# Turns by squares and DRAM, a full-width second product and merged transfers in a macaron block of two layers

## The chip, the cores and the metric

The kernel runs on one core of one Trainium2 chip. The metric is the device time of one execution in microseconds; a lower time is better. A core has a matrix engine (PE, whose weight loads are listed as PEld), a vector engine (DVE), a scalar engine for activation functions (ACT), a general engine (POOL) and an engine that in this kernel issues all transfers (SP). Each engine works through its own instructions in order and waits on semaphores for the others.

## The reference

The input x is 8 batches of 256 tokens of 128 numbers, all in float32. Six residual blocks follow one another, each behind a layer norm:

```
x = x + 0.5 * soft_moe(norm(x))
x = x + linear_attention(norm(x))
x = x + 0.5 * soft_moe(norm(x))
x = x + 0.5 * ternary_ffn(norm(x))
x = x + favor_attention(norm(x))
x = x + 0.5 * ternary_ffn(norm(x))
```

- `soft_moe` normalizes again and forms logits of each token against 16 x 64 slots. A softmax over the tokens of a batch mixes the tokens into slots ("dispatch"); each of the 16 experts computes `(gelu(slots Wg + bg) * (slots Wu + bu)) Wd + bd` on its 64 slots of each batch; a softmax over all 1024 slots of a token mixes the experts' outputs into the token ("combine").
- `linear_attention` has 16 heads of 8, `elu + 1` as feature map, sums of keys and values over the tokens of a batch, a division and a projection.
- `favor_attention` has 16 heads of 8 with 32 random features each: a projection, a maximum over the 32, an exponential, sums over the tokens, a division and a projection.
- `ternary_ffn` widens to 512, takes silu times a linear part, then two layers of 512 x 512 with gelu, then goes back to 128.

## The kernel before

**Tiling.** x stays in SBUF, with tokens on the 128 partitions and two tiles (TT = 2) for each batch. The eight batches form two groups of four (`group`, L1366). In a group two layers follow one another: `dispatch` for each batch, `experts` over the 16 experts for all four batches at once, `combine` for each batch and, in the first layer, `linear` for each batch. Behind that come `glu` (the ternary network, for batches in pairs), `favor` and `glu` again. A matmul in float32 appears in the profile as two instructions; a turn of a block as one.

**Order of the work.** The kernel is written as steps. A step (`step`, L90) names its cost on the engines that may run it, its reads and writes, and the buffers it takes. A planner (`Plan.place`, L123) runs once, when the program is built: it goes through the steps with these costs, chooses engine, start and buffer slot for each, and so fixes one order of instructions for each engine. Its priorities are the amount of PE work ahead of a step, moved by a list of numbers (`SHIFTS`), with the second group behind the first by a constant. The two groups thus interleave on every engine. Where the planner sees PE idle for over 0.7 us, it puts some multiplications by an identity before the next step (`idle`, L1399). SP issues every transfer in the planned order; a transfer that has to wait holds all that stand behind it on SP.

**Turning a tile.** Matmuls contract over partitions, so tiles with tokens on partitions must be turned, that is, transposed. The kernel has two ways. `flip` (L375) lets PE turn a block of 128 x 128 into PSUM, from where ACT or DVE evacuates it (`evacuated`, L384 on DVE, L382 on ACT). `squares_turned` (L440) lets DVE turn every square of 32 x 32 (L446), writes the tile to DRAM with one transfer (the spill, L449) and reads it back with four, one for each set of 32 partitions, so that the squares come to stand in their turned places (the placing, L455). Before the change, `linear`, `glu` and one of the operands of `favor` are turned by squares; the normalized y of `dispatch`, the maxima in `dispatch`, the attention output in `project` (L888) and the sums in `favor` go by `flip`.

**dispatch (L594).** It normalizes x into y and turns y (`transposed`, L465), with scale and bias of the norm put on in the evacuation (L493 on ACT, L495 on DVE). `replicated` (L573) spills y to DRAM with four transfers (L579) and reads it back with four (L586) in another order of tokens, copied to each set of 32 partitions. Eight products give the logits (L615); the maximum over slots of a token is folded from them (L632, L708). Then PE turns the maxima, DVE reduces them (L719), PE spreads them over all partitions, and an evacuation gives `mb`, which POOL subtracts from the logits (L737) before the exponential (L743). The softmax over tokens has its own path (L649 to L678) and ends in the products that fill the slots (L691).

**experts (L749).** For each expert, SP fetches one row of weights (L764, 384 KB) into one of four buffers; for every second expert it also fetches the bias bd of the pair with two transfers (L767). The first products (L787) give gate and up part (L793 on ACT, L798 on DVE). The second product (`back`, L818) works on a pair of experts together: each matmul has 64 columns of the array for 64 slots, the even expert on the first half of the array and the odd one on the second, and the bias addition (L830 on DVE) writes its result where `combine` reads it. The results share their memory with the slots. It stands one pair behind the first products.

**combine (L852)** gathers with eight products of 129 columns for each tile (L859).

Of the kernel before, what the change touches and what calls it, by code (L numbers as in the profile page):

```python
# [13 lines left out]
P = 128  # L14

SHIFTS = (
    -2751, -1692, -1691, -12195, -784, -1588, -17523, -441, -1660, -895, -929, -659, -543, -591,
    -517, -633, -219, -357, -610, -370, -144, -340, -138, -261, -103, -124, -149, -112, -87,
    328, -365, -173, -179, -134, 14, 40, -32, 136, -182, -43, -162, -672, 13, -20, 26, 13, -393,
    -13, -49, 76, 108, 25, -337, -106, -98, -405, -124, -14, 106, -15, -91, -232, -26, -141, 72,  # L20
    179, -149, -60, -56, -94, -291, -910, -397, 168, -109, -149, -2, -601, -150, 12, -21, -762,
    -20, -100, 231, -63, -522, -971, -639, -490, -1134, 34, -143, -240, -1126, 30, 98, 272,
    -229, -245, 48, 535, -647, -666, -418, 7, 144, -282, -73, 220, 168, 36, -1118, -353, -720,
    -886, -200, -34, 24, 100, 11, -24, 70, 30, -50, -121, 47, 25, 9, -51, 143, -939, -125, -300,
    -662, -491, -371, -203, -437, -21, -285, -479, -125, 412, 243, 49, 284, 369, 566, -147,
    -339, 157, 267, -173, -269, 162, -518, -492, 53, 116, -414, -523, -222, -451, -400, -304,
    -82, 145, -77, -134, -36, -467, -865, -141, -372, -407, -524, -134, 12, 58, -154, 246, 41,
    -111, 22, 62, -756, -131, 38, -435, -1331, -683, -948, -2046, -2339, -2000, -3450, -2514,
    -3516, -3317, -2307, -1684,
# [187 lines left out]
def macaron_kernel(ctx: ExitStack, tc: tile.TileContext, i: dict, out: bass.AP):  # L217
# [222 lines left out]
    def squares_turned(z, n, cells, dst, out):  # L440


        flat = lambda: z()
        there = dram.tile([P, n // 32, 32], F32, tag=f"t{len(turns)}", name=f"t{len(turns)}")
        turns.append(there)
        step({"DVE": 58 + 1.07 * n}, lambda _: nc.vector.transpose(z(), z()), cells, cells)  # L446

        def spill(_):
            nc.sync.dma_start(there.rearrange("p k j -> p (k j)"), z())  # L449
# [10 lines left out]
        step({"SP": 475}, spill, cells, [there.name], lag=1.5 * n)  # L460
        step({"SP": 2000}, place, [there.name], out, lag=2.5 * n)
# [3 lines left out]
    def transposed(y, n, affine=False, squares=False):  # L465

        yt = Buf("k1" if n == TT else "k2", (P, n * P))
        if squares:
            squares_turned(
                lambda: y.ap[:, 0:n].rearrange("p t d -> p (t d)"), n * P,  # L470
                [(y, t) for t in range(n)], lambda: yt.ap, [yt],
            )
            return yt
# [1008 lines left out]
```

## Time and profile before

| | |
|---|---|
| median of 3 runs | 741.02 us (740.77 to 742.02) |
| the profiled execution | 743.85 us, span 742.1 us |
| PE busy | 728.8 us, 98% |
| DVE busy | 517.2 us, 70% |
| ACT busy | 410.7 us, 55% |
| POOL busy | 306.1 us, 41% |
| bytes moved | 62.34 MB, 30.6% of the 16 DMA engines' time |
| mean granted TensorE clock | 0.998 |

"Busy" is time in which an engine executes. PE's matmuls are pipelined: the mean of one (275 ns with 128 columns) is longer than the distance between two starts, so a group's price is read from the start of the group to the start of the next. "Idle before" is time for which the engine stood before an instruction of that line, with whoever ended it. The planner's orders of both programs are known before anything runs, and with them the number of instructions of each kind and what stands between two of them on an engine.

### The profile page before, as it was taken

To read this page: it belongs to the slowest core of one execution; us is meant where nothing else is said; L and a number is where in the kernel's file an instruction comes from. 1 tells how busy PE (TensorE), PEld (TensorE's weight loads), DVE (VectorE), ACT (ScalarE), POOL (GpSimd) and SP (SyncE) were. 2 spreads that over 40 slices of the span, in tenths; PEclk is the share of its full clock that TensorE was granted. 3 is DMA by queue.
4 is the path that set the end of the run, shared out by engine and by line. 5 is a ranking of instruction groups with operands and counts; after the bars stand their busy time and mean duration, and the time that the engine had idled before them with its cause. 6 is when DMAs were issued, how large, how long until landed. Compare 5 with 4: busy or idle time off the path is not lost.

```text
span 742.1 us, 15296 instructions
## 1 busy us (share of the span) xinstructions
PE 728.8 (98%) x5814; PEld 609.5 (82%) x5814; DVE 517.2 (70%) x1103; ACT 410.7 (55%) x774; POOL 306.1 (41%) x419
## 2 busy tenths in 40 slices
PE   8999999998999999999999999999999999999998
PEld 7878888997889988889878879788687677878787
DVE  6999965577868798975564274455998978855442
ACT  4889967257665577884553240433555664363331
POOL 7989446133427752459910022000745545211000
PEclk9999999999999999999999999999999999999999
DMA  5553432333330526333631210200344244120100
GB/s 143 150 140 118 139 93 94 109 81 97 126 114 2 146 83 197 99 94 119 171 99 52 85 29 1 57 0 15 78 114 95 42 118 81 32 60 14 42 1 29
DMA packets 102105, 62.34 MB, mean 84 GB/s; under 512 B 73104, under 2 KB 88848, under 8 KB 102032
## 3 DMA queue, kind: packets, MB, share of 16 engines
q1 hardware_dynamic: 102032, 61.36, 30.6%
q8 instruction: 46, 0.75, 0.4%
q14 instruction: 27, 0.22, 0.1%
HBM read 49.80 MB, written 11.53 MB: 83 GB/s over the span
## 4 chain that ended last, share of the span: by engine, by line
PE 87%; DVE 5%; DMA 3%; SPq 2%; issue 1%; POOL 1%; ACT 1%; POOLq 0%
PE ps L1077 27%; PE ps L787 14%; PE ps L818 8%; PE ps L859 8%; PE ps L691 6%; PE ps L615 4%; PE ps L1177 4%; PE ps L1147 4%; PE ps L1150 4%; PE ps L375 2%; DMA we<-in_We 1%; PE ps L1256 1%; DVE k L632 1%; PE ps L1307 1%; PE ps L1341 1%; PE ps L907 1%
## 5 line engine op out<-in xcount | busy, mean ns | idle before, releaser
L787 PE MATMUL ps<-slots,we 128*128 128x256 f32 x512 | 121.8, 384 | 4.0 <-DMA we<-in_We 2.3
L787 PEld LDWEIGHTS ps<-slots,we 128*128 128x128 f32 x512 | 94.7, 191 | 20.1 <-issue 5.2
L1077 PE MATMUL ps<-comb,slots 128*128 128x256 f32 x448 | 103.1, 381 | 0.0
L1077 PE MATMUL ps<-comb,comb 128*128 128x256 f32 x448 | 102.5, 381 | 0.0
L1077 PEld LDWEIGHTS ps<-comb,slots 128*128 128x128 f32 x448 | 83.6, 190 | 15.4 <-issue 3.9
L1077 PEld LDWEIGHTS ps<-comb,comb 128*128 128x128 f32 x448 | 83.6, 190 | 13.6 <-issue 2.5
L737 POOL TENSOR_TENSOR comb<-comb,k 128x1024 f32<-128x1024 f32 x32 | 75.1, 2369 | 33.5 <-DVE k L384 14.0
L793 ACT ACTIVATE k<-ps,small 128x256 f32<-128x256 f32 x128 | 56.5, 475 | 48.4 <-PE ps L787 46.1
L382 ACT COPY k<-ps 128x512 f32<-128x512 f32 (+2 forms) x55 | 28.5, 519 | 93.8 <-PE ps L1077 83.1
L670 POOL TENSOR_TENSOR comb<-comb,sm 128x1024 f32<-128x1024 f32 x32 | 60.9, 1911 | 41.4 <-DVE sm L665 41.4
L798 DVE SCALAR_TENSOR_TENSOR k<-ps,small,k 128x256 f32<-128x256 f32 x128 | 57.2, 475 | 29.2 <-ACT k L793 28.5
L412 POOL TENSOR_SCALAR sm<-sm 128x2 f32<-128x2 f32 x52 | 10.0, 193 | 153.1 <-DVE sm L406 140.1
L657 ACT ACTIVATE comb<-comb,sm 128x256 f32<-128x256 f32 x128 | 63.3, 497 | 13.7 <-PE ps L691 7.4
L1091 DVE TENSOR_TENSOR comb<-ps,k 128x512 f32<-128x512 f32 x48 | 32.9, 687 | 49.0 <-PE ps L1077 25.5
L818 PEld LDWEIGHTS ps<-we,k 128*64 128x64 f32 x1024 | 55.3, 137 | 9.2 <-issue 4.7
L615 PE MATMUL ps<-k,seT 128*128 128x256 f32 x256 | 61.7, 383 | 0.8 <-DVE k L495 0.5
L818 PE MATMUL ps<-we,k 128*64 128x128 f32 x1024 | 62.2, 275 | 0.0
L691 PE MATMUL ps<-comb,k 32*128 32x256 f32 x1024 | 59.9, 380 | 0.1
L859 PEld LDWEIGHTS ps<-slots,comb 128*128 128x128 f32 x512 | 58.4, 192 | 1.5 <-issue 1.3
L859 PE MATMUL ps<-slots,comb 128*128 128x129 f32 x512 | 59.6, 276 | 0.0
L1099 ACT ACTIVATE comb<-comb 128x512 f32<-128x512 f32 x48 | 30.0, 629 | 51.0 <-DVE comb L1091 50.8
L691 PEld LDWEIGHTS ps<-comb,k 32*128 32x128 f32 x1024 | 51.4, 185 | 5.6 <-issue 1.4
(144 smaller groups left out, 1303.7 us busy)
## 6 DMA issues: line engine op xcount, KB each, us to landing
we<-in_We SPq DMA_DIRECT2D x64, 384.0 KB, 3.8
k<-y SPq DMA_DIRECT2D x64, 128.0 KB, 2.9
t<-comb SPq DMA_DIRECT2D x8, 512.0 KB, 2.8
k<-t SPq DMA_DIRECT2D x32, 128.0 KB, 3.5
y<-k SPq DMA_DIRECT2D x64, 32.0 KB, 1.9
we<-in_bd SPq DMA_DIRECT2D x64, 32.0 KB, 3.6
t<-k SPq DMA_DIRECT2D x16, 128.0 KB, 1.7
k<-t SPq DMA_DIRECT2D x64, 32.0 KB, 2.3
```

What stands on the lines that cost most here:

```text
L615: mm(pl.ap[:, j, :], seT[:, 2 * u + j].rearrange("p k s -> p (k s)"), yt.ap, start=True, stop=True,)
L657: nc.scalar.activation(ex.ap[:, 4 * h + j, :], comb.ap[:, 4 * h + j, :], AF.Exp, bias=mx.ap[:, j : j + 1], accum_out=mx.ap[:, 4 + j : 5 + j],)
L670: nc.gpsimd.tensor_tensor(ex.ap[:, part], ex.ap[:, part], mx.ap[:, 8:12].unsqueeze(2).to_broadcast([P, 4, N]), ALU.mult,)
L691: mm(po.ap, yr.ap[rows, c, :], ex.ap[rows, :, 32 * c : 32 * c + 32], start=(c == 0), stop=(c == N // 32 - 1), tile_position=(32 * a, 0),)
L737: nc.gpsimd.tensor_tensor(raw, raw, mb.ap.unsqueeze(1).to_broadcast([P, 4, N]), ALU.subtract)
L787: mm(pe.ap[:, m, :], we.ap[:, ts(2 * m + c, P)], sl.ap[:, j, k, :, 0:S], start=True, stop=True,)
L793: nc.scalar.activation(ga.ap, pe.ap[:, 0, :], AF.Gelu, bias=bg[:, e, c : c + 1])
L798: nc.vector.scalar_tensor_tensor(ht.ap[:, c, :], pe.ap[:, 1, :], bu[:, e, c : c + 1], ga.ap, ALU.add, ALU.mult,)
L818: mm(po.ap[S * k : S * k + S, q, :], hts[k].ap[:, c, ts(q, S)], wes[k].ap[:, ts(4 + c, P)], start=(c == 0), stop=(c == 1), tile_position=( ...
L859: mm(po.ap[:, t, 0 : D + 1], comb.ap[:, j, ts(t, P)], eo()[:, j, q, 0 : D + 1], start=(j == 0), stop=(j == NJ - 1),)
L1077: mm(bank.ap[:, o], w(k)[:, c, ts(o, P)], rhs().rearrange("p (c n) -> p c n", c=2)[:, c, :], start=(start and o + c == 0), stop=(stop and ...
L1091: nc.vector.tensor_tensor(C(i, k)(), bank.ap.rearrange("p o n -> p (o n)"), other(), ALU.add)
```

## The change

- `back` works on one expert at a time: four products with all 128 columns of the array, for two of the four batches at a time. Its result stands with the slots of two batches on two halves of the partitions, so it goes to a buffer `moved`, and two transfers bring the halves to the place that `combine` reads. The bias bd is part of the weights' row (448 KB), repeated on every partition.
- `replicated` spills with one transfer and reads back with one.
- Four more kinds of turn go by squares and DRAM: in the second layer's dispatch, y (with scale and bias put on afterwards) and the maxima (a turn of squares, a reduction over 32 slots, a spill of 4 KB, a transfer that gives every partition all 1024 partial maxima, a reduction over four); in `linear`, the attention output; in `favor`, the sums. The first layer's dispatch keeps its turns on PE.
- The planner's costs and lags for the transfers have other values, and `SHIFTS` is another list; the orders on all engines differ from the start.

The diff, without `SHIFTS`:

```diff
-    def squares_turned(z, n, cells, dst, out):
+    def squares_turned(z, n, cells, dst, out, by=None):
         there = dram.tile([P, n // 32, 32], F32, tag=f"t{len(turns)}", name=f"t{len(turns)}")
         turns.append(there)
-        step({"DVE": 58 + 1.07 * n}, lambda _: nc.vector.transpose(z(), z()), cells, cells)
+        done, at = ([by], lambda: by.ap) if by else (cells, z)
+        step({"DVE": 58 + 1.07 * n}, lambda _: nc.vector.transpose(at(), z()), cells, done)
         def spill(_):
-            nc.sync.dma_start(there.rearrange("p k j -> p (k j)"), z())
+            nc.sync.dma_start(there.rearrange("p k j -> p (k j)"), at())
...
-        step({"SP": 475}, spill, cells, [there.name], lag=1.5 * n)
-        step({"SP": 2000}, place, [there.name], out, lag=2.5 * n)
+        step({"SP": 335}, spill, done, [there.name], lag=1.1 * n - 850)
+        step({"SP": 2400 + 0.7 * n}, place, [there.name], out, lag=1.2 * n - 300)
...
         def spill(_):
-            for k in range(4):
-                nc.sync.dma_start(
-                    spilled[b].rearrange("i (t k) d -> i k t d", k=4)[:, k],
-                    y.ap[32 * k : 32 * k + 32],
-                )
+            nc.sync.dma_start(spilled[b].rearrange("i (t k) d -> k i t d", k=4), y.ap)
         def spread(_):
-            for a in range(4):
-                nc.sync.dma_start(yr.ap[32 * a : 32 * a + 32], spilled[b])
+            nc.sync.dma_start(
+                yr.ap, spilled[b].unsqueeze(0).to_broadcast([4, 32, N // 32, D])
+            )
...
-    def dispatch(b, sl):
+    def dispatch(b, sl, last):
-        yt = transposed(y, TT, True)
+        yt = transposed(y, TT, True, squares=last)
...
+        if last:
+            def turn_max(_):
+                nc.vector.transpose(pm.ap[:, 0], pm.ap[:, 0])
+            def slot_max(_):
+                nc.vector.tensor_reduce(
+                    mn.ap, pm.ap[:, 0].rearrange("p (c s) -> p c s", s=32), AX.X, ALU.max
+                )
+            def spill(_):
+                nc.sync.dma_start(there, mn.ap)
+            def spread(_):
+                nc.sync.dma_start(
+                    mr.ap.rearrange("p a n -> p (a n)"),
+                    there.rearrange("p c -> (p c)").partition_broadcast(P),
+                )
+            def token_max(_):
+                nc.vector.tensor_reduce(
+                    mb.ap.rearrange("p (c i) -> p c i", i=32),
+                    mr.ap.rearrange("p a (i c) -> p c i a", i=32), AX.X, ALU.max,
+                )
...
-                nc.sync.dma_start(we.ap[:, 0 : 6 * P], i["We"][e])
-                if e % 2 == 0:
-                    for k in range(2):
-                        nc.sync.dma_start(
-                            we.ap[S * k : S * k + S, 6 * P :],
-                            i["bd"][e + k].partition_broadcast(S),
-                        )
+                nc.sync.dma_start(we.ap, i["We"][e])
...
-        def back(j, wes, hts):
-            po = ps_(BG, P)
+        def back(e, we, ht):
+            j, k = e // 2, e % 2
+            po = ps_(NB, P)
+            moved = Buf("k1", (P, NB, P))
             def down(_):
-                for q in range(BG):
+                for r in range(NB):
                     for c in range(2):
-                        for k in range(2):
-                            mm(
-                                po.ap[S * k : S * k + S, q, :], hts[k].ap[:, c, ts(q, S)],
-                                wes[k].ap[:, ts(4 + c, P)], start=(c == 0), stop=(c == 1),
-                                tile_position=(0, S * k),
-                            )
+                        mm(
+                            po.ap[:, r, :], ht.ap[:, c, ts(r, P)], we.ap[:, ts(4 + c, P)],
+                            start=(c == 0), stop=(c == 1),
+                        )
             def biased(_):
                 nc.vector.tensor_tensor(
-                    eo()[:, j, :, 0:D], po.ap,
-                    wes[0].ap[:, 6 * P :].unsqueeze(1).to_broadcast([P, BG, D]), ALU.add,
-                )
+                    moved.ap, po.ap, we.ap[:, 6 * P :].unsqueeze(1).to_broadcast([P, NB, P]),
+                    ALU.add,
+                )
+            def place(_):
+                for h in range(2):
+                    nc.sync.dma_start(
+                        eo()[S * k : S * k + S, j, h::2, 0:D], moved.ap[S * h : S * h + S]
+                    )
...
     def project(b, oh, w):
-        step({"PE": flips(TT)}, turn, [oh], [pt], takes=[ot])
-        evacuated(lambda: ot.ap, lambda: pt.ap.rearrange("p t c -> p (t c)"), [pt], [ot], N)
+        squares_turned(
+            lambda: oh.ap.rearrange("p t d -> p (t d)"), N, [oh], lambda: ot.ap, [ot]
+        )
...
-        step({"PE": flips(2)}, turn_sums, [kvm], [pkt])
-        evacuated(
-            lambda: kv.ap, lambda: pkt.ap.rearrange("p a (c n) -> p a c n", c=4), [pkt], [kv], N
-        )
+        squares_turned(
+            lambda: kvm.ap.rearrange("p a n -> p (a n)"), N, [kvm],
+            lambda: kv.ap.rearrange("p a c n -> p (a c n)"), [kv],
+        )
```

## The prediction

> **What bounds the kernel now.** I read the engine table of the page first, then the chain, the groups of instructions, the waits of the matmul queue, the stretches of 10 us, and last the timelines of PE and of SP around the one large gap.
>
> ```profile
> span 742.1 us, 15296 instructions
> PE 728.8 (98%) x5814; PEld 609.5 (82%) x5814; DVE 517.2 (70%) x1103; ACT 410.7 (55%) x774; POOL 306.1 (41%) x419
> PE 87%; DVE 5%; DMA 3%; SPq 2%; issue 1%; POOL 1%; ACT 1%; POOLq 0%
> ```
>
> PE is busy 728.8 of 742.1 us and is 87% of the chain that ended last: a microsecond taken from PE after the start-up is worth nearly a microsecond, as long as nothing new makes PE wait. The groups show what the changed matmuls cost now.
>
> ```profile
> L818 PE MATMUL ps<-we,k 128*64 128x128 f32 x1024 | 62.2, 275 | 0.0
> L1177 PE MATMUL ps<-w3T,comb 128*128 128x128 f32 x256 | 30.1, 275 | 0.0
> L375 PE MATMUL ps<-ident,k 128*128 128x128 f32 x112 | 23.5, 288 | 3.2 <-DVE k L708 1.1 <-POOL k L420 0.7 <-DVE k L1000 0.5
> L375 PE MATMUL ps<-ident,sm 128*128 128x128 f32 x32 | 6.5, 285 | 0.0
> L446 DVE STREAM_TRANSPOSE k<-k 128x256 f32<-128x256 f32 (+1 forms) x24 | 12.5, 522 | 0.8 <-POOL k L420 0.5
> L719 DVE TENSOR_REDUCE sm<-ps 128x2 f32<-128x256 f32 x16 | 6.5, 409 | 0.1
> L649 DVE TENSOR_REDUCE sm<-comb 128x4 f32<-128x1024 f32 x32 | 38.1, 1200 | 0.0
> ```
>
> The means of PE overlap one another, so I price by starts: on the timeline of PE the 32 instructions of L818 that begin at 127.85 us end where the next group begins, at 129.74 (1.9 us, or 0.059 each), the 32 of L1177 at 729.95 give way at 733.52 (3.57 us, 0.112 each), and two turns of L375 at 160.55 give way at 160.77 (0.22, 0.11 each). A full-width product with 128 columns thus costs twice a half-width one: the pairs on the two halves of the array already ran side by side.
>
> The one large wait of PE after the start-up, and what it cost:
>
> ```profile
> 179.13 1.03 PE L787 MATMUL ps<-slots,we 128*128 128x256 f32 x4
> 182.32 1.46 PE L787 MATMUL ps<-slots,we 128*128 128x256 f32 x4 [2.17 <-DMA we<-in_We]
> 184.00 1.92 PE L787 MATMUL ps<-slots,we 128*128 128x256 f32 x4
> ```
> ```profile
> 168.02 3.04 SPq L579 DMA_DIRECT2D y<-k  x4
> 171.56 2.58 SPq L455 DMA_DIRECT2D k<-t  x4
> 174.24 0.55 SPq L764 DMA_DIRECT2D we<-in_We  x1
> 174.83 1.16 SPq L767 DMA_DIRECT2D we<-in_bd  x2
> 176.03 0.58 SPq L764 DMA_DIRECT2D we<-in_We  x1
> ```
> ```profile
> 180.00:190.00 10.00, 7.83 (x36) 6.73 (x36) 6.22 (x17) 4.82 (x10) 2.70 (x3) 0.83 0.47 117
> ```
>
> The expert weights were issued late, behind a file of small transfers on SP; PE stood for 2.17 us, and then the granted clock fell (the stretch's 0.83, against 1.00 in its neighbours). The four instructions of L787 at 184.00 took 1.71 us until the next group, twice the 0.86 of four elsewhere. At 0.83 over 10 us the loss is 1.7 us, so this one late transfer cost 2.2 + 1.7 = 3.9 us.
>
> **The change, part by part.**
>
> *Turns taken from PE.* The changed program as built issues 64 turns on L375 instead of 144: 80 fewer (16 of the second layer's y, 32 of its maxima, 16 of the outputs, 16 of the FAVOR+ sums). 80 x 0.11 = 8.8 us less on PE. All lie after 130 us, where PE has next to no idle time; the start-up, which waits for data, keeps its turns. Their PSUM evacuations (32 of 128x256, 0.37 us on ACT or 0.41 on DVE) go as well.
>
> *Second product.* 32 x 32 half-width instructions (32 x 1.86 = 59.5 us; 1.82 when two stand together, 1.90 alone) become 64 x 8 full-width ones. At 0.112 each this is 57.3 us. Gain 2.2 us; if every one of the 64 groups pays a start like the 0.08 us between the 1.90 and the 1.82 (32 starts more, 2.6 us) it is a loss of 0.4, and 3.5 us is the other end (all old groups at 1.90). I take -1.9.
>
> *Transfers merged.* Per dispatch, eight DMAs (y<-k four, k<-y four) become two; the 64 small DMAs of bd go into the weights' row (448 KB instead of 384). SP saves 64 x 0.55 (bd) + 48 x 0.6 (y<-k) + 48 x 0.46 (k<-y) = 86 us of issuing. The transfers that stood ahead of the weights at 168 us were of these. It adds 24 spills at 0.33 (8 us), 96 placings at 0.64 (61 us), 16 DMAs of the maxima (6 us) and 128 DMAs that place the moved second product (0.43 to 0.63 each by the weights' and y's rows, I take 0.5 by the nearer y: 64 us). SP ends 53 us busier: 561 DMAs for 457. Its queue waits in order, so each spill holds what follows until DVE has turned its block, and each placing until the spill has landed.
>
> *Weights.* A weight buffer was freed two by two, after the pair's product; now after each expert. Before, the fetch for the expert after next could begin only some 3.5 us of expert work ahead of use, against 3.8 us to land; now three experts' products (3 x 4.3 us) stand between. Together with the shorter file on SP this removes the stall at 180 us (-3.9), but SP is busier in just that stretch, so I count only half: -2.0. Bounds -4.1 (both PE waits for weights, 2.17 and 0.18, with the clock's loss) and 0.
>
> *DVE, ACT, POOL.* DVE gets 24 transposes (0.43), 8 transposes and 8 reductions of the maxima (0.43, 0.41), 8 wide reductions (1.2) less 8 old ones, and 64 additions of 256 for 32 of 512 (+4 us); some 22 us in all, 70% to 73%. It is hidden by PE's other group except where DVE is full (25 to 50 us), which gets none of it. ACT gets 27 more table loads (101 for 74, 1.28 us each): 35 us, 55% to 60%, beside PE. If that cover fails at one load in ten, 3.5 us. POOL issues the same kinds; cost nothing, hidden likewise.
>
> *Longer chains.* The page's transfers (last number: median us from issue to landing):
>
> ```profile
> t<-k SPq DMA_DIRECT2D x16, 128.0 KB, 1.7
> k<-t SPq DMA_DIRECT2D x64, 32.0 KB, 2.3
> y<-k SPq DMA_DIRECT2D x64, 32.0 KB, 1.9
> ```
>
> A turn took PE 0.22 us and an evacuation 0.4. By squares it is 0.43 (DVE) + 1.7 (spill lands) + 3 x 0.64 + 2.3 (last placing lands) = 6.4 us. In the built order PE has, between the linear attention's products and the projection, 9.6 to 13 us of other work (counted with the prices above); they need 0.95 for the division and 6.4, so 7.4. Between the FAVOR+ sums and products it has 10 to 20 us. Between the last second product and the first combination, 4.3 to 6.9 us against about 0.4 + 0.5 + 0.5 + 1.9 = 3.3. The cover holds everywhere, by 1 to 6 us, more behind the sums; a queue on SP eats it. From 115 to 200 us of PE's work SP has some 62 us of issues in 86 (48 placings of turns 31, 32 of the second product 16, 13 weights 6, the rest 9), where its timeline from 150 to 213 us shows some 38 in 63. New waits: nothing at least (all covered), 16 us at most (four stalls like the one above); I take +2.5, less than one such stall, because the old turns by squares made PE wait just 0.32 us in all.
>
> Sum: -8.8 - 1.9 - 2.0 + 2.5 = -10.2. The profiled execution took 743.85 us (span 742.1 and 1.75 around it), 2.8 above the median of 741.02; from it 733.6, and against the median 730.8. I say 731.
>
> [...] The trace's row has the fall after an idle of 2.17 us, at the end of a thin stretch. [...]
>
> **Rivals.**
> - *SP's queue becomes the bound (slower).* Place: the projections and second dispatches of either group, where SP issues 72% of the time. Price 3.9 us a stall; with 12.7 us saved it decides from four stalls on. At six: 741 - 12.7 + 23 = 751; at four or five, 744 or 748. For it: the late fetch at 176 us was such a file, and spills now wait on DVE there. Against: PE waited for DMA 2.7 us in the whole run.
> - *The work leaves PE and half the time stays.* Two stalls, or ACT's loads show: 741 - 12.7 + 8 = 736.
> - *All is covered and the weights' waits go entirely:* 8.8 + 3.5 + 4.1 = 16.4 less, 725.
> - *The second product saves nothing* (starts eat it): 733; a size, not a sign, so inside the first case.
>
> **How the numbers follow.** The likeliest, 731 (727 to 735), 0.44; half the gain, 736 (735 to 739), 0.18; everything, 725, 0.14; SP as the bound 0.24, of which 0.04 ends within 0.2% of 741 (1.5 us, about what a measurement of this kernel can tell from no change) and 0.20 above. Faster 0.76, same 0.04, slower 0.20. The range leaves out a tenth below and a tenth above: 721 to 744, that is from the case with everything into the slow rival at four stalls.
>
> **What would show it.** PE busy about 11 us less with a busy share still 97% or more; L375 x64, the new second product x512 near 57 us by starts; no PE wait on the weights; granted clock 1.00 in all stretches. Wrong: PE's idle time over 25 us, with waits on the placings of turns or on weights issued behind them, and stretches at less than full clock between 120 and 330 us.

## The result, and the profile after

The changed kernel took 848.23 us (median of 4 runs, 844.21 to 849.86) where the kernel before took 740.89 us on the same chip. The ratio is 1.144, with an interval of 1.139 to 1.149. I had forecast 731 us, with 744 as the upper end; it is 107 us slower than before instead of 10 us faster.

The engine table, the granted clock and the chain that ended last, from the page of the changed kernel:

```profile
span 848.1 us, 14505 instructions
PE 740.9 (87%) x5210; PEld 618.7 (73%) x5210; DVE 534.9 (63%) x1143; ACT 446.8 (53%) x801; POOL 315.9 (37%) x427
PEclk9987899999978997989969999999999999999999
PE 57%; DMA 21%; POOL 6%; SPq 6%; DVE 5%; issue 2%; ACT 2%; ACTq 0%; DVEq 0%; POOLq 0%
```

PE has 604 instructions fewer than before (5210 for 5814), and is still busy for longer (740.9 us for 728.8), because the clock is below full in the first half: the row PEclk, a digit for each fortieth of the span in tenths of full speed, shows less than 9 in eight of its first 21 slices and in none behind them. Its idle time went from 13 us to 107. DMA was 3% of the chain that ended last and is now 21%. What PE waited for, in the view of waits:

```profile
PE ps L814 <- DMA we<-in_We: 23.0, 10, 5.8
PE ps L691 <- DMA k<-y: 20.3, 1, 20.3
PE ps L615 <- ACT k L496: 15.2, 5, 7.9
PE ps L934 <- DMA k<-t: 15.2, 6, 8.0
PE ps L847 <- DVE k L825: 13.5, 4, 7.0
PE ps L891 <- DMA slots<-k: 5.6, 3, 4.3
```

(The columns are the total in us, the number of waits and the longest.) Weights, the read of y back, the placings of turns, the moves of the second product: each is a transfer that the change touched. The waits of L615 on ACT and of L847 on DVE are one step removed: ACT waits there 35.5 us for placings of y, to put scale and bias on, and DVE 17.6 us for the maxima, which come through DRAM.

The largest single wait, 20.3 us, shows the first cause best. The timeline of SP, and the chain of waits in the same stretch:

```profile
40.37 0.51 SPq L584 DMA_DIRECT2D k<-y  x1
40.97 0.53 SPq L581 DMA_DIRECT2D y<-k  x1
51.73 0.51 SPq L584 DMA_DIRECT2D k<-y  x1
52.33 0.53 SPq L581 DMA_DIRECT2D y<-k  x1
61.94 0.51 SPq L584 DMA_DIRECT2D k<-y  x1
```
```profile
40.97 10.71 DMA y<-k
...
52.33 9.53 DMA y<-k
...
61.94 8.66 DMA k<-y
```

SP is not busy here: it issues for 0.5 us and then waits 10. The spill of y (128 KB) is issued at 40.97, lands 10.71 us later, and only then can the read back be issued; the next spill goes out right behind that read and lands 9.53 us later. The last read takes 8.66 us. Before, each quarter of a spill landed after 1.9 us and each quarter of a read after 2.9 (medians).

### The profile page after: what moved, and what is told of

It is laid out like the page before. It is cut to its first block, busy times and chain, and to the rows that moved or that the text cites. A ratio compares the mean times of both kernels' runs of the same rounds, so it can differ in the third digit from the quotient of the medians.

```text
span 848.1 us, 14505 instructions
## 1 busy us (share of the span) xinstructions
PE 740.9 (87%) x5210; PEld 618.7 (73%) x5210; DVE 534.9 (63%) x1143; ACT 446.8 (53%) x801; POOL 315.9 (37%) x427
## 2 busy tenths in 40 slices
DMA packets 145367, 83.28 MB, mean 98 GB/s; under 512 B 99985, under 2 KB 131089, under 8 KB 145297
## 4 chain that ended last, share of the span: by engine, by line
PE 57%; DMA 21%; POOL 6%; SPq 6%; DVE 5%; issue 2%; ACT 2%; ACTq 0%; DVEq 0%; POOLq 0%
PE ps L1104 22%; PE ps L814 8%; DMA k<-t 5%; DMA k<-y 4%; PE ps L847 4%; DMA y<-k 4%; SPq L455 4%; PE ps L691 4%; PE ps L1204 3%; PE ps L891 3%; DMA t<-k 3%; PE ps L1177 3%; DMA we<-in_We 3%; PE ps L1174 3%; POOL comb L670 2%
## 5 line engine op out<-in xcount | busy, mean ns | idle before, releaser
L814 PE MATMUL ps<-slots,we 128*128 128x256 f32 x512 | 125.4, 395 | 23.8 <-DMA we<-in_We 23.0
L814 PEld LDWEIGHTS ps<-slots,we 128*128 128x128 f32 x512 | 97.5, 198 | 41.9 <-issue 14.9
L691 PE MATMUL ps<-comb,k 32*128 32x256 f32 x1024 | 64.8, 404 | 21.4 <-DMA k<-y 20.3
L615 PE MATMUL ps<-k,seT 128*128 128x256 f32 x256 | 67.4, 412 | 17.5 <-ACT k L496 15.2
L847 PE MATMUL ps<-we,k 128*128 128x128 f32 x512 | 67.5, 282 | 13.5 <-DVE k L825 13.5
L847 PEld LDWEIGHTS ps<-we,k 128*128 128x128 f32 x512 | 65.0, 197 | 18.8 <-DVE k L825 15.9
L691 PEld LDWEIGHTS ps<-comb,k 32*128 32x128 f32 x1024 | 54.9, 200 | 29.8 <-issue 23.0
L615 PEld LDWEIGHTS ps<-k,seT 128*128 128x128 f32 x256 | 49.7, 204 | 29.2 <-ACT k L496 16.9
L891 PE MATMUL ps<-slots,comb 128*128 128x129 f32 x512 | 61.9, 280 | 5.6 <-DMA slots<-k 5.6
L382 ACT COPY k<-ps 128x512 f32<-128x512 f32 (+2 forms) x43 | 22.4, 525 | 73.4 <-PE ps L1104 67.5
```

What stands on the lines that cost most here:

```text
L615: mm(pl.ap[:, j, :], seT[:, 2 * u + j].rearrange("p k s -> p (k s)"), yt.ap, start=True, stop=True,)
L691: mm(po.ap, yr.ap[rows, c, :], ex.ap[rows, :, 32 * c : 32 * c + 32], start=(c == 0), stop=(c == N // 32 - 1), tile_position=(32 * a, 0),)
L814: mm(pe.ap[:, m, :], we.ap[:, ts(2 * m + c, P)], sl.ap[:, j, k, :, 0:S], start=True, stop=True,)
L847: mm(po.ap[:, r, :], ht.ap[:, c, ts(r, P)], we.ap[:, ts(4 + c, P)], start=(c == 0), stop=(c == 1),)
L891: mm(po.ap[:, t, 0 : D + 1], comb.ap[:, j, ts(t, P)], eo()[:, j, q, 0 : D + 1], start=(j == 0), stop=(j == NJ - 1),)
```

## The experiments

Except where it is said, each kernel keeps the order of the instructions of the one that it was made from, so that only the edit differs. A letter in an expectation names a theory within that expectation; in the text I call them by name. Where no interval is given the time is that of one execution, so that 2 us between two such kernels is about the least that can be read (seven executions of the kernel before on one chip lay between 739.06 and 743.23 us).

**The merged transfers of y, undone and alone.** In the change, the spill and the read back of y are one transfer each, and each has a dimension of 4 ahead of its rows:

```
-            nc.sync.dma_start(spilled[b].rearrange("i (t k) d -> k i t d", k=4), y.ap)
+            for k in range(4): ...            # four spills of 32 partitions, as before
-            nc.sync.dma_start(
-                yr.ap, spilled[b].unsqueeze(0).to_broadcast([4, 32, N // 32, D])
-            )
+            for a in range(4):
+                nc.sync.dma_start(yr.ap[32 * a : 32 * a + 32], spilled[b])
```

Both parts of the edit, then the second part alone, then the opposite edit on the kernel before:

> The changed kernel, but with y spilled by four transfers and read back by four, as before the change; the planner's costs are left, so that the order of all other instructions stays. Theory A (the merged transfers of y run on a few of the 16 DMA engines, land after 8 to 10 us, and hold what stands behind them): the 20 us wait of PE in front of the first slots goes, most of the 107 us that PE stood goes, and the time is 728 to 745 us. Theory B (SP has too many transfers to issue; these six more for each dispatch make it worse): 840 us or more. Theory C (the moved second product or the longer turns are what PE waits for): 810 to 850 us, with PE's waits on the placings left.

> The changed kernel, but only the read-back of y by four transfers; the spill stays one. Theory A: the read is the 512 KB part, so it carries most; the spill of 128 KB in one transfer should cost about a quarter as much: 735 to 765 us. Theory B: 840 us or more. Theory C: 810 to 850 us.

> The kernel before, with nothing changed but y spilled by one transfer and read back by one, the order of everything else kept. Theory A: the same transfers hold up SP here too: 790 to 850 us, with PE waiting in front of the first slots for the read-back as in the changed kernel. Theories B and C: 735 to 745 us, since SP issues 96 transfers less and the second product and the turns are the old ones.

With both in fours the change took 797.68 us (795.24 to 803.07, ratio 1.0753, 1.0722 to 1.0784); with the read alone in fours 792.25. The kernel before with both merged took 786.66, 46 us above the 740.95 of the kernel before on that chip. So the merging costs some 50 us in either kernel, and that is about half of the 107. The other half is not explained by it: I had expected at most 745 and 765 us of the first two, and both missed. To split the spill as well as the read gained nothing more. In the kernel before with merged transfers the waits are not even on y:

```profile
PE ps L784 <- DMA we<-in_We: 34.4, 6, 18.9
```

One wait of 18.9 us for weights, which the edit does not touch. They were issued at 65.61 us and after, 2 us behind two merged reads.

**Engines or size.** A merged read may be late because it is 512 KB in one piece, or because its slowest dimension is 4. Two transfers of 256 KB, each with a slowest dimension of 2, tell these apart:

```
-            for a in range(4):
-                nc.sync.dma_start(yr.ap[32 * a : 32 * a + 32], spilled[b])
+            for a in range(2):
+                nc.sync.dma_start(
+                    yr.ap[64 * a : 64 * a + 64],
+                    spilled[b].unsqueeze(0).to_broadcast([2, 32, N // 32, D]),
+                )
```

> The kernel before, order of the instructions kept, with only the read of y back merged: two transfers of 64 partitions each (each gives the same 32 rows to two blocks) for four of 32; the spill keeps its four transfers. Theory A (a transfer whose slowest dimension is 4 or 2 runs on only so many of the 16 DMA engines, and the time to land follows from that): two engines for 256 KB each; as four engines took 8.7 to 9 us for 512 KB, each of these takes about as long, and where both share the two engines longer, against 2.9 us for each of the four before. 12 reads back, so at least as slow as the kernel with spill and read merged, of which the read was the larger half: 765 to 800. Theory B (the time comes from the size of a transfer, 512 KB in one piece): 256 KB then lands in about half of 8.7 us, 4.4, beside one another; the loss is at most a third of the +46 us, 741 to 756.

It took 867.56 us: smaller transfers than the merged ones, and slower by another 81 us than the kernel with both merged. (There are 16 reads back, not the 12 that the expectation names.) The size falls as the cause, and my own upper end of 800 was far too low. The chain of waits of this kernel:

```profile
48.48 10.94 DMA projT<-in_projT
...
65.10 22.33 DMA k<-y
...
95.70 22.11 DMA we<-in_We
```

Four of these reads are issued in a file from 63.30 us on; one of them, issued at 65.10, lands after 22.33 us, and a fetch of weights issued behind others lands after 22.11 us, against 3.8 before. The packets in the trace give the sum. In this kernel 254 packets of 4 KB ran from 65.65 to 86.88 us, 169 ns each on average: 254 x 0.169 / 2 = 21.5 us, the measured 21.2. In the changed kernel 128 packets of 4 KB ran from 53.53 to 60.03 us at 197 ns: 128 x 0.197 / 4 = 6.3 us, measured 6.5; and from 63.23 to 70.05 at 207 ns: 6.6, measured 6.8. The windows view shows the same by the busy share of the 16 DMA engines (the last number but one):

```profile
53.50:60.00 6.50, 0.00 (x0) 0.00 (x0) 0.56 (x1) 1.26 (x6) 6.50 (x4) 0.68 0.26 85
```

While a merged read runs 0.26 x 16, some 4 engines, are busy; in the kernel before, between 25 and 35 us, 0.65 x 16 or 10.4. For the kernel with reads in twos the packets give 254 x 0.169 / 21.2, some 2 engines. So a merged read with a slowest dimension of 4 ran on 4 of the 16 DMA engines and one with 2 on 2, and in these stretches such transfers shared the same few: what was issued behind them waited for these. That is also why the spill, only 128 KB, took 9.53 us: it was issued 0.6 us behind a merged read, and its packets began only as the read's ended, at 59 to 60 us. A transfer on all engines waited for the few too. In the kernel with reads in twos three fetches of weights (128 packets each) follow four such reads: 336 of the 384 packets, seven eighths, started between 101.7 and 110 us, and the rest only from 115.4 us on. Fourteen engines of sixteen were free for them, two were not.

**The other half: the new trips through DRAM.** From the change with the read in four (792.25 us, order kept) I left out trips. These kernels leave data where it should have been moved and so compute something else, with the same work on PE. For instance the moves of the second product, where DVE then writes to the slots at once:

```
-                    moved.ap, po.ap, we.ap[:, 6 * P :]...
+                    eo()[:, j, 2 * k : 2 * k + 2, 0:D], po.ap, we.ap[:, 6 * P :]...
-                for h in range(2):
-                    nc.sync.dma_start(eo()[S * k : S * k + S, j, h::2, 0:D], moved.ap[S * h : S * h + S])
```

and for a turn, `nc.vector.transpose` straight into its destination, with no spill and no placings.

> The changed kernel with the read-back of y in fours and, at the same places in every engine's order, without any of the new trips: DVE writes the second product straight to its end place (wrong slots), the turns of the second layer's y, of the outputs and of the sums are written by DVE alone (squares turned, not moved to their places), and the maxima are not spilled or spread (a token's maximum is taken over one partition's slots). It leaves the moving of data out, so its output is not the reference's; PE does all its work. Theory A (the new trips are what PE waits for in the 52 us that remain over the kernel before): 722 to 738 us, 731 being the forecast for a change whose trips are all covered. Theory D (the order of the work, planned with new costs and a new list of shifts, is what leaves PE idle, whatever the trips take): 770 us or more.

> As the changed kernel with the read-back in fours, but DVE writes the second product straight to its end place (the slots come to stand wrongly) and the 128 moves are not issued; order kept. Theory A, if the moves carry most by filling SP's queue (128 x 0.6 us, in front of weights and placings): 755 to 770 us; if the turns carry most: 783 to 793 us. Theory D: 788 to 795 us.

> As the changed kernel with the read-back in fours, but the second layer's y and the outputs of the linear attention are turned by DVE in squares alone, without spill and placing (80 transfers less; the squares stay in their places, so what is computed from them is not the reference's); order kept. Theory A, if these turns carry most, since they stand in the chain between the layers: 750 to 770 us; if the moves carry most: 780 to 793 us. Theory D: 788 to 795 us.

> Of the new trips only that of the maxima is left (with the read-back of y in fours, the moves and the other new turns left out as in the run without any of them); order kept. DVE waits in order for the maxima's 512 KB, 8.9 us once in the trace with all trips, and PE behind it. If this trip holds PE by itself: 10 to 25 us above the run without any trip; if it waits only because SP's queue is full of the others: within 4 us of it.

> The changed kernel with the read of y back in four, its order kept, and of the new trips only the 128 transfers that move the second product to its slots; the turns of y, outputs and sums end after DVE's transposes and the maxima stay where they are (the output is not the reference's). Without any trip this took 734.0, with all trips 792.2, and leaving the moves out of the latter saved 34. Theory C1 (each trip costs its own length, whatever else SP does): 734 plus about 34, 762 to 772. Theory C2 (the trips are late because they stand behind one another in SP's queue): the moves alone are cheap, 736 to 750. Theory F (64 KB from SBUF to SBUF are slow by themselves): long waits of the combinations on the slots, 770 or more.

> The same kernel without trips, but with the turn of the FAVOR+ sums through DRAM as in the change. It has 10 to 20 us of other work of PE behind it and a free queue on SP. Theory C (a trip with cover in work of PE and in SP's queue costs nothing): 733 to 736 against 734.0 without. Theory E (every trip through DRAM ends as a wait): two groups, two waits of 4 us and more, 742 or more.

| trips kept | us | above none |
|---|---|---|
| none | 733.98 | |
| sums | 736.40 | 2.4 |
| moves | 740.97 | 7.0 |
| maxima | 751.46 | 17.5 |
| maxima, y, outputs, sums (no moves) | 757.95 | 24.0 |
| moves, maxima, sums (no y, no outputs) | 764.59 | 30.6 |
| all | 792.25 | 58.3 |

(The kernel before took 739.38 us on the chip of the runs with none, with the maxima alone, without moves and without y and outputs, and 740.95 on that of the other three, so 1.6 us of the costs of sums, moves and all may be the chip's.) With no trips the order that the change brings is a good one, 5.4 us below the kernel before on the same chip; the page of that kernel:

```profile
span 732.3 us, 14089 instructions
PE 714.1 (98%) x5210; PEld 606.5 (83%) x5210; DVE 526.5 (72%) x1143; ACT 443.9 (61%) x801; POOL 316.0 (43%) x427
```

It runs the same 5210 PE instructions as the changed kernel in 26.8 us less of busy time (714.1 against 740.9), at a granted clock of 0.998 for 0.951, and with 18 us of idle time instead of 107. The theory that the order leaves PE idle whatever the trips take falls with it.

The trips do not add up. Alone, sums, moves and maxima cost 2.4, 7.0 and 17.5; y and outputs add about 4 to the maxima and sums (757.95 - 751.46 - 2.4). That is 31 us, and together they cost 58.3. The moves cost 7.0 alone and 34.3 on top of the rest; y and outputs 4 without the moves and 27.7 with them. So some 27 us come only when they run together, and the question was through what. The price of the maxima holds their reduction too: the one over the spread maxima takes 2.08 us, the one that stands in its place without the trip 1.21.

**What they share: SP's queue or the DMA engines.** First the whole change in its lightest form: y spilled as one transfer of 128 partitions in its own layout, the read in four.

```
-            nc.sync.dma_start(spilled[b].rearrange("i (t k) d -> k i t d", k=4), y.ap)
+            nc.sync.dma_start(spilled[b].rearrange("p t d -> p (t d)"), y.ap.rearrange("p t d -> p (t d)"))
 ...
+                    yr.ap[32 * a : 32 * a + 32].rearrange("i (t k) d -> i t k d", k=4),
+                    spilled[b].rearrange("(k i) t d -> i t k d", k=4),
```

> The whole change, its order kept, with y spilled as one transfer of 128 partitions in y's own layout and read back in four, as in h1_lighter. Theory A: with the read in four, only the spill still runs on few engines (128 KB, slowest dimension 4); on 16 engines it lands in about 2 us, and 12 to 16 dispatches start 1 to 2 us sooner each where PE waits for them: 775 to 790, below the 792.2 with the read alone in four. Theory G (the rest is the trips, and the spill's engines don't matter any more): 790 to 794.

789.83 us (788.73 to 792.20; ratio 1.0655, 1.0625 to 1.0685). That is at the border of both expectations, and does not tell them apart: the spill's few engines matter by some 2 us at most once the read is in four. From this kernel the weights were then issued by another engine, and at last the moves too:

```
-                nc.sync.dma_start(we.ap, i["We"][e])
+                nc.gpsimd.dma_start(we.ap, i["We"][e])     # or nc.scalar
 ...
-                    nc.sync.dma_start(eo()[...], moved.ap[...])
+                    nc.gpsimd.dma_start(eo()[...], moved.ap[...])   # last of the three; weights by nc.scalar
```

> The kernel f9_light_change, order kept, with the 64 fetches of the expert weights issued by POOL instead of SP, so that they no longer stand behind spills and placings that wait. Theory C3 (the weights are late because SP's queue is in order; PE waited 18.1 us for them in ten waits, and the clock fell after the longer ones): those waits go, and with the clock's loss 20 to 30 us: 760 to 772 from 789.8. Theory H (the weights are late because the DMA engines are busy with the other transfers): PE still waits 12 us or more for them, 780 to 792. Theory I (POOL is held up by the fetch's own wait for a free buffer, as SP was, and its work comes late): other waits on POOL appear, 790 or more.

> The same with the fetches issued by ACT. Theory C3: the waits for weights go, 760 to 775. Theory H: 780 to 792. Theory I: ACT stands in its order behind fetches that wait for a free buffer, and PE waits for ACT's work; ACT is 56% busy against POOL's 41%, so more than by POOL: 790 or more.

> The kernel f9_light_change, order kept, with the 64 fetches of the weights issued by ACT and the 128 moves of the second product by POOL, so that SP has only the turns, the maxima, the dispatches and the outputs left. With the weights alone on another queue the PE waits on weights went (18.1 to 2.2 and 3.8 us) and as many on the placings of turns came in their place, with no gain. Theory C3 (the common queue of SP is what makes whichever transfer comes last late): SP has 79 us of issues less, the placings come in time, 755 to 775. Theory L (the chains of the two groups through DRAM are longer than the work of the other group that should cover them, on whatever queue they are issued): the waits move on once more, to the moves or to DVE's work behind the maxima, 782 to 795.

794.54, 792.93 and 791.28 us: no gain in any. The waits of PE for weights went or shrank (18.1 us to 3.8, 2.2 and 7.9). Ahead, the light change; behind it, with the weights issued by ACT:

```profile
PE ps L816 <- DMA we<-in_We: 18.1, 10, 5.5
...
PE ps L936 <- DMA k<-t: 5.3, 4, 2.7
```
```profile
PE ps L936 <- DMA k<-t: 17.6, 5, 5.6
...
PE ps L816 <- DMA we<-in_We: 2.2, 3, 1.1
```

What weights no longer cost, the placings of turns cost now. With 192 issues taken from SP (the third of the three kernels) the chain still has spills and placings of 5 to 6 us that landed in about 2 in the kernel before (medians 1.7 and 2.3). So the weights and moves in SP's queue, part of what my slow rival blamed, do not hold this kernel. Two things limit this. POOL pays for what it issues (the 128 moves are 76.7 us of its time), so in that run one load took the place of another. And SP's order is not out of it: between 150 and 420 us the issuing of placings on SP is 9.6% of the chain in the light change and 11.0% with the weights issued by ACT; in one place of the light change SP issues placings for 6 us (266.87 to 272.88) before the read of the maxima goes out. No run took the placings off SP. The last run took bytes away, not issues:

```
+                n = 6 * P + D if len(had) < 8 else 16
+                had.append(e)
-                nc.sync.dma_start(we.ap, i["We"][e])
+                nc.sync.dma_start(we.ap[:, 0:n], i["We"][e, :, 0:n])
```

> The kernel f9_light_change, order and queue kept, but after the first 8 fetches of weights only the first 16 columns of each row are fetched (the products use what lies in the buffers, the output is not the reference's): some 24 of 83 MB less, and no other transfer stands behind a 448 KB one. Theory H (the DMA engines are crowded: busy 0.52 instead of 0.34 between 150 and 450 us, and transfers that take 2 us alone land after 5 to 7 there): the waits on weights go and the placings land in about 2 us, 745 to 772. Theory L (the chains are long even with every transfer at its own length): as with the weights on another queue, 780 to 795.

768.88 us, 21 less than the light change. The stretch from 150 to 450 us of the kernel before, of the light change, of the light change with weights issued by ACT and of the one with small weights (columns: us, busy time of PE, PEld, DVE, ACT and POOL, granted clock, busy share of the DMA engines, GB/s):

```profile
150.00:450.00 300.00, 296.15 (x2491) 254.72 (x2490) 210.58 (x473) 179.28 (x352) 126.92 (x172) 0.99 0.34 98
```
```profile
150.00:450.00 300.00, 252.13 (x1777) 216.89 (x1777) 203.79 (x446) 171.79 (x332) 121.05 (x150) 0.94 0.52 142
```
```profile
150.00:450.00 300.00, 255.00 (x1791) 223.74 (x1790) 203.63 (x451) 172.43 (x337) 121.39 (x150) 0.93 0.52 143
```
```profile
150.00:450.00 300.00, 270.23 (x1914) 237.32 (x1913) 213.38 (x468) 178.44 (x347) 121.62 (x154) 0.97 0.33 83
```

In the light change the DMA engines are busy 0.52 of this stretch, not 0.34, whichever queue issues; with small weights they are back at 0.33, and PE is busy 18 us more within the same 300. What the load does to a transfer's landing, in the same stretch of the kernel before, of the light change (two lines) and of the one with small weights (the last number is the median):

```profile
t<-k SPq DMA_DIRECT2D x8, 128.0 KB, 1.7
```
```profile
t<-k SPq DMA_DIRECT2D x20, 128.0 KB, 3.5
...
k<-t SPq DMA_DIRECT2D x84, 32.0 KB, 2.3
```
```profile
t<-k SPq DMA_DIRECT2D x20, 128.0 KB, 1.9
```

The spills take twice as long in the light change; the placings keep their 2.3 us. So about 21 of the 49 us that the light change is slower come with the load on the DMA engines, and 28 stay with the transfers near their own length. I take it that the chains themselves are longer than the work that should cover them, the maxima's (17.5 alone) above all; the runs do not show it one by one, and SP's order may have a part. Small weights also take away the waits on weights, but the runs with the weights on another queue did that too and gained nothing, so I put the 21 down to the load, which is argued and not isolated. Whether it acts by a few crowded engines or by all of them no run tells apart; the trace speaks for all, as every transfer of the light change leaves the same 16 completions in it (9744 for 609 transfers), where the 32 merged ones of the changed kernel leave 5 each (8624 for 561 transfers).

**Two kernels planned anew.** In these the planner made a new order with the edit in it.

> The changed kernel with the read of y back in four transfers, and the maxima of the second layer turned by TensorE as before instead of by squares and DRAM; the order is made anew with that. Theory C (the new trips share SP's queue and land too late): the maxima's trip alone cost 17.5 us above the kernel with no trips, so 792 less 10 to 25 us: 767 to 782. Theory D (what remains is due to the order, not to the trips): another order from the same planner, with the other trips as they are, falls by less than 8 us: above 784.

> The kernel h1_lighter, planned anew with the FAVOR+ sums turned by squares and DRAM as in the change (16 turns of TensorE fewer, 16 x 0.11 = 1.8 us; eight DVE transposes, two spills and eight placings more). Theory C (trips cost where SP's queue is full, not by themselves): this trip stands behind 10 to 20 us of other work of PE and SP has 112 transfers fewer, so 1.8 us less than h1 or even with it: 734 to 741. Theory E (every trip through DRAM ends as a wait, wherever it stands): two more stalls of 4 us and more: 745 or more.

The first took 792.20 us. The waits on DVE behind the maxima went (11.8 us to 0.2 on L846, both against the kernel with the read alone in fours), the waits on weights rose (15.6 to 25.2), and the plan has 66 more matmuls on the identity that only fill gaps. The second took 777.33 us (ratio 1.0477, 1.0459 to 1.0496); its groups show why:

```profile
L1388 PE MATMUL ps<-ident 128*128 128x128 f32 x346 | 43.3, 283 | 1.6 <-POOL ident masks.py:199 1.6
```

346 filling matmuls where the kernel before has 86: the new plan had left gaps on PE, at some 0.11 us by starts for each of the 260, 29 of the 36 us. I read both as verdicts on the order, not on the trip, and neither settles what its expectation asked. The run with the sums alone in a kept order (736.40, 2.4 above none) answers the second; that is about the 1.8 us that 16 turns cost on PE, so that even this trip, with 10 to 20 us of cover, shows no gain that could be read.

**A version that beats both.** The kernel before, its order kept, with the biases in the weights' rows and the light spill:

> The kernel before, its order kept, with two parts of the change done so that every transfer still begins with 32 or 128 partitions as its slowest dimension: the 64 small transfers of the biases go into the weights' rows, and the spill of y is one transfer of 128 partitions with rows of 2 KB (read back in four, whose rows of 512 bytes are put in order on the way). Theory A (merging cost nothing as such, the few engines did): SP issues 112 transfers fewer, the PE wait of 2.17 us on the weights goes or shrinks, with its half clock: 736 to 741. Theory B (any merging of these transfers makes them land late): the dispatches wait as in the kernel with merged transfers: 755 or more. [...]

737.78 us (737.54 to 738.33) against 741.65 on the same chip; ratio 0.9952, 0.9937 to 0.9966. Its timeline of SP where the kernel before had its one large wait, and the stretch behind it:

```profile
167.13 3.60 SPq L455 DMA_DIRECT2D k<-t  x4
170.82 1.02 SPq L763 DMA_DIRECT2D we<-in_We  x2
171.89 2.53 SPq L582 DMA_DIRECT2D k<-y  x4
```
```profile
180.00:190.00 10.00, 10.00 (x101) 8.83 (x102) 9.90 (x22) 8.18 (x20) 1.39 (x2) 1.00 0.27 74
```

The weights are issued at 170.82 us instead of 174.24 and 176.03, PE does not wait for them, and the clock of the stretch is 1.00 for 0.83. The gain of 3.9 us equals the price that the prediction had put on that one stall (2.2 + 1.7), but by chance. Five of the seven executions of the kernel before on that chip had a granted clock of 0.999 or 1.000, and their median is among them, so the medians hardly have the clock's 1.7 us in them. From one profiled execution to the other (743.85 to 737.61) 6.2 us went: PE's idle time fell by 3.7 us (13.3 to 9.6), which is the wait of 2.17, one of 1.17 for ACT at 105.39 us and some smaller ones, and its busy time by 2.5, in which the clock's part lies.

## Why the prediction was wrong

**Turns taken from PE, and the second product: right in work, half of it in time.** L375 is there 64 times. With the trips left out PE is busy 14.7 us less than before (714.1 for 728.8). Of this some 1.3 is 12 filling matmuls fewer (86 to 74, at 0.11 each) and some 1.7 the slow stretch at 184 us; nearly 12 remain, where I had 8.8 + 1.9 = 10.7. But the time fell by 5.4 us only, as PE also stood more, 18 us for 13. The new second product runs at 0.112 us each where nothing stops it: 32 of them in 3.58 us on the chain of the light change.

**Transfers merged: the step that failed first.** It counted what SP saves on issuing (86 us less there, 53 more in net) and took for granted that a merged transfer lands like its parts. The term should have been the landing time: 512 KB on 4 engines, 8.7 us to land (6.3 to 6.6 of it packets) instead of 2.9, with spills and weights held up behind on the same engines. It is some 46 to 56 us, and I had a gain.

**Longer chains, +2.5 with a bound of 16: the step that failed second.** The 7.4 us for a turn were worked out from the rows of before, 1.7 for the spill and 2.3 for the placings. Those rows were measured at a DMA share of 0.34. The change moves 83.28 MB for 62.34, and most of the added 21 lie in the stretch from 150 to 450 us; there a spill's median was 3.5 us instead of 1.7 and 8 of 22 took over 4, where none of 10 had before; the longest on the chain:

```profile
259.65 7.16 DMA t<-k
```

(from the chain of the light change). The placings kept their 2.3. The cover of "1 to 6 us" that I had found was thinner than this. The maxima had no chain of their own in my sum at all: they cost 17.5 us by themselves, with 512 KB that land after 4.4 us (median, light change), DVE in order behind them, and a reduction over strided maxima that took 2.08 us (L737) where I had priced 1.2 by L649. The bound of 16 was four stalls, chosen from one stall's price and not from what could come late; with the read in four the term measured 58.

**The weights' stall: there, but wrong here.** The version above shows that the stall can be removed by lighter transfers. Its price was right for the profiled execution; the sum took it, with the clock's 1.7 us, from a median of executions that hardly had the clock's part. And instead of -2.0 the weights became the largest wait, 23.0 us in ten waits, since they ran behind merged transfers and in a crowd. Freeing the buffers earlier did not help a transfer that lands late.

**DVE, ACT, POOL at nothing: held in the main.** Without trips PE was 98% busy, with nearly all of these kinds of work still there. It did wait 3.4, 2.7 and 1.7 us for DVE at L844, L993 and L928, where its longest wait for DVE before was 1.1 us; some of the missing gain is there.

**The clock.** I counted with the row, by which the clock fell after 2.17 us of waiting. The granted clock averaged 0.951 for 0.998 before, and took 26.8 us of PE's busy time (740.9 for the 714.1 of the same instructions without trips), so new waits did cost more than their own length. Some of these waits were long, the longest 20.3 us, but the runs with few trips have shorter ones. Without any trip:

```profile
PE ps L844 <- DVE k L822: 3.4, 2, 3.2
```
```profile
351.90:355.30 3.40, 3.40 (x18) 3.40 (x18) 2.02 (x6) 0.00 (x0) 3.40 (x3) 0.50 0.19 33
```

The wait of 3.20 us ends at 351.2 us, and from 351.9 the clock is at half for 3.41 us. A wait of 2.95 us with the moves alone and waits of 2.77 and 3.00 with the sums alone were followed by half clock for as long; one of 2.67 without trips was not. So waits of 2.17 and of 2.77 to 3.20 us cost clock in these runs and one of 2.67 did not: what a wait costs could not be told from its length alone.

**The rivals.** The slower one had the right sign and the right signs to look for (waits on weights and placings, PE idle over 25 us, stretches below full clock), but its cause was not borne out: taking 64 and 192 issues off SP's queue changed nothing, though the placings stayed in it. At 751 it was also sized by a count of stalls on SP; there was no rival in which the DMA engines are the bound, although the transfers were half of the change.

What stays open: how the 28 us that are left with small weights divide among the maxima, the moves, the turns of y and SP's order of issuing, and in what order a planner would have to place them; the new plans that were tried brought other losses.

## What to carry to other kernels

Before two transfers are merged, look at the slowest dimension of both sides: here transfers with 4 and with 2 on one side ran on 4 and on 2 of the 16 DMA engines, and what was issued behind them waited as well (weights landed after 22.11 us where the median before was 3.8). Price a transfer three times, by its issue, by its landing and by its bytes on the engines that it shares; a landing time from a quiet profile need not hold where the change itself fills the stretch (here the spills' went from 1.7 to 3.5 us and the placings' stayed at 2.3). When PE's wait moves from one transfer to the next as each is relieved and the time stays (here 18.1 us on weights, then 17.6 on placings, at 789.83 and 792.93 us), the wait shows only what came last; look then for what the transfers share.

## What was not expected of the hardware

- Two transfers of 256 KB were far slower than one of 512 KB: 16 reads of two such made the kernel before 126 us slower, the merged ones together with merged spills 46 us. Here the engines in use, 2 for 4, outweighed size and number of transfers.
- A transfer with rows on all engines was as late as the slowest of them: 384 KB of weights landed 22.11 us after their issue, behind reads that kept two engines busy while seven eighths of the packets had long gone (336 of 384 started by 110 us, the rest from 115.4 on).
- SP was also held in issuing: in the kernel with reads in twos a single issue of WkT's load stands for 5.45 us on SP's timeline (39.17 us), where the same issue takes 0.68 in the kernel before with merged transfers.
- A transfer from SBUF to SBUF of 64 KB landed after 2.1 us (median, light change), about as long as the spills (128 KB, 2.0) and placings (32 KB, 2.2) of turns in the same run, and 128 of them cost 7.0 us alone.
